# New engine sequences for a four-layer graph network kernel, and its bound checks moved into the planned graph

## The chip, the cores and the metric

The kernel runs on one core of a Trainium2 chip. The metric is the device time of one execution in microseconds; lower is better. The core has five engines that work side by side and meet through semaphores: PE (TensorE) multiplies matrices, DVE (VectorE) and ACT (ScalarE) do elementwise work, POOL (GpSimd) does small elementwise work and issues some DMAs, and SP (SyncE) issues the other DMAs. Each engine executes its own instructions in the order in which the program lists them. So the order in which the program is written decides who waits for whom.

## The reference

Sixteen batches of `x`, each 1024 nodes by 256 features in float32, and one `adj` matrix of 1024 by 1024 integers shared by all batches. Four layers, each with a norm in front and a residual:

```python
h = jnp.maximum(_layernorm(x, axis=-1), 0.0)
x = x + layer(h, adj, ...)

# layers 0 and 1: one-head graph attention
h = jnp.matmul(inp, W)
e = leaky_relu(e_src[:, :, None] + e_dst[:, None, :])     # e_src = h @ a1, e_dst = h @ a2
e = where(adj == 0, -1e9, e)
out = relu(softmax(e) @ h)                                # layer 1: elu, another slope

# layer 2: eight-head dot attention with the same mask, then
x = layernorm(x + t); f = relu(x @ w1 + b1) @ w2 + b2; x = layernorm(x + f)

# layer 3: graph attention with four heads of 64, elu
```

## The kernel before

The kernel has a fast path and a general path. The fast path computes softmax without subtracting the row maximum. It keeps track of extreme values while it works (`gat_seen`, `inv_seen`, `degree`, `below`); at the end it tests them against bounds, counts the broken ones into `bad`, and the program runs the general path only if `bad` is above zero (L2013 and L2014). With these inputs it is not run.

**Stages.** A stage is one layer of one batch. Stages are interleaved by a fixed list, so that a stage that needs much of DVE and ACT runs beside one that needs much of PE. In its steady part the list repeats layer 2 of batch b, layer 1 of b+1, layer 3 of b, layer 0 of b+2, once per batch.

**What a stage does.** `way_in` normalises a batch's rows, 128 nodes at a time, turns them on PE (`transpose_rows`, L1096 and L1099) and multiplies them by the layer's weights (`project`, L1103). Layers 0 and 1 (`gat_item`) form attention weights `p` on DVE (L1366) from a row `r`, a column `e` and the mask, and multiply them with the values `v` on PE (L1383, accumulator `av`). Layer 2 (`dot_item`) goes in groups of four heads by 128 keys by 512 queries: the scores on PE (`sc`, L1599), two exps on ACT (L1613), two multiplications by the mask on DVE (L1621), the values on PE (`acc`, L1630). The softmax sums need the weights of two groups added: a DMA that POOL issues adds one `pe` tile onto another in SBUF (`gather`, L1647, 1 MB), and PE sums the result (`totals`, L1660). Layer 3 (`pair_item`) forms two heads' weights at a time on DVE (L1445) and multiplies on PE (L1479 and, for the sums, L1503). After layer 2 comes `feed_forward`: for 128 nodes at a time DVE takes mean and variance (L1050, L1051), POOL adds epsilon and takes the power -1/2 in `root` (L1054, L1055, on 128 numbers), ACT scales (L1758), and PE turns and multiplies. `root` of the other norms is L1080 and L1081.

**Three forms of matmul.** Wide ones use the whole array (128*128: L1096, L1103, L1383). Scores use 32 rows and 128 columns (32*128), four heads beside each other. Values and sums of layers 2 and 3 use 128 rows and 32 columns (128*32).

**Memory.** Tiles sit in rings (`Ring`, `Hold`). PSUM has three places of two banks (`u`) and two of one bank (`acc`); one score group takes two of the `u` places. A ring's place comes free when the operations named in `ends` are done.

**The order.** Nothing is executed in the order in which the Python code creates it. Each piece of work is an `op` with an engine, a cost in microseconds, what it comes after, which ring places it takes and ends. The DMA queue of the gathers counts as a sixth engine, `QUEUE`. `forward` plays all operations on a model of the engines: at each step it takes the operation that can begin earliest, and among those within `SLACK` of 0.5 us the one with the lowest rank. The string `RANKS` holds one rank per operation, three characters each. The order in which the model plays is the order in which instructions are written out. A change of matmul form costs extra on PE (`SWITCH`), and `held` keeps a POOL operation from beginning while a DVE operation with two operands in SBUF runs:

```python
if o.eng == PE and o.form != form:
    cost, form = cost + SWITCH[o.form], o.form
if o.tiles:
    held[o.eng] = at + cost - BEFORE_END
```

SP's queue carries, in program order: the loads of `x` (`load_x`, L653), the edges of `adj` at the start (L724), the weights (L676), the rows `kept` (stored at L1312) and `r` (loaded at L1323 and L1327) of the graph attention stages, and the stores of the result (L1578). At the start ACT's queue carries the first layer's weights.

Of the kernel before, what the change touches and what calls it, by code (L numbers as in the profile page):

```python
# [26 lines left out]
F32 = mybir.dt.float32  # L27
BF16 = mybir.dt.bfloat16
U8 = mybir.dt.uint8
# [6 lines left out]
P = 128  # L36
# [11 lines left out]
    "#+;#TX#$I#U9#U3#&X#%h#WX#)4#Wc#&>#$b#U)##w##W$5o##o##Z##D##b#$'#$-##t##$#$:##r##y##G##Q#$F#$>#/4#$N#$R##x#%-#%^"  # L48
    "#$o#'S#'T#&F#&a#%g#&$#'%#&{##T#$|##?##@#%F#SZ##B#%+##>##S#$f##c##M##a##L##]##9##v##i##z##|##u##^#$@#$)##n#$0#$4"
    "##U#oi#-@##V#sX##F##X#$^##=##_#%e##P#)h##{#$<##q#$`#/3#$&#$P##m#$3#$8#$J#$,#$9#$K#$1#*e#%r##%##j#$a#&4$0;#Cy$0r"  # L50
    "#RB#Cx#%|#']#**#&@#)g#([#'q#%m#&]#&7#%v##8#$=##}#$G##-#$L#$_#$j#$M##)#$E##p#$]$$T#'?#%a$Mo#%5#$n#$U#%L#%9#%}#%R"
    "##(#$C#%%#$c#%8##Y#&L#%7#xt#%S#'V#]n#%l#$5$%C#%V#%E#0W#%0##l#&+#$i#&,#%n#(o#)v#)V#D,#%t#$v#$r#$S#%$#%##%'#$O#$d"
    "#$H#$6#)z##4#K5#$+#&I#%?#%Y#(8#YI#(A#<Z#$A#&;#$l#%x#&1#Au#$7#(s#%,#$;#%.#%T#%z#%O#&:#DW#d-#&Q#&A#)W#%s#'H#DU#'P"
    "#'E#&0#(2#(I#(4#'r#*d#e6#&=#,6#k8#&m$Fk$Pc#($#$x#>b#$w#$Z#%3#5Q#$T#&8$@{##J#%X##O#Gr#({#%:#'K#$h#&c#'8##,#&[#%="
    "#T+#$u#&`#V9#%&#'-#%*#JZ#SB#%/#%i##C##5#%w#us##2##H##N#$s#$.#$k##e##;#$e#')#%P#&l#%<##d#$*#$##vC#%K#XB#*|#$B#%G"
    "##A$/b#&6##1#%`#&D#((#%]#%I#%{#&%##0#%_#%Q#&9#&##&)#D=##7#FF$&r#&C#%d#&.##6#)0#&B#+4#O)##3##[#&Y#%@#&g#;b$&?#e'"
    "#4O#%2#&Z#&*#(y##/#%j$/i#&&#'&#di#&p#&/#&f#&M#&|#'.#('$5w#'*#(%#&N#$2#'6#&3#&d#&R#&K#&U#&o#&V##.#DD#&E#&q#M9#'="
    "#&<#&n#eH#'D#',#w'$0(#'X#'C#&z#'J#&h#'@$6t#U@#'[#';#'A#%;#(-#'x#a}#DE#kw#'W#%p#'_#N[#&r#(>#Sm#&u#)G$.4#)P$.3#&e"
    "$Ip#'d#ma#tD#);$Pa$Ph$PQ$K?#&i#'I#&s#'N#&v#'2#&j#%A$D+#&P#&H#0A#%k#(D$JC#'p#'>#'a#&x#&_$JO#G;#O/#'5#'L#%1#'k#0>"
    "$78#(P#ip#'e#'7#kv#P)#d`$Ms$1j#'g#(G#Pd#(l#)@#(E$?$#(c#0.#'w#'s#(p#'G#)E#'}#''#(^#(&#'|#(6#UK#(/$@J#'#$@O#'y#()"  # L60
    "#ku#$Q#'v#$/#Il#.W#B1#(:#(.$>1#)3#4/#Ix#4.#(5#(L$;V$>D##k#(1$9##'u#))#(d#)%#)^#*=#)_#)t##g#'R#'j#(##(,#'U#(9#'i"
    "#(n#(B#(V#(W#&'#(*#'m#*n#)8#)1#(}#;4#)y$$:#(x#C,#(i#(Y#(h#(_#(z#)m#(U#&?#)b#(g#(k#*K#(j$*_#(f#J@#*2#)F#Ah#,[$*9"
    "#*,#*7#-z#<c#)*$LG#)=#)<#++#)M#*:#-(#(v#)B#*+#)i#:q#*1#+9#2y#)?#)Q#+J#)D$$z#*3#,,#*}#)p#)U#;Y#'h#)a#$Y#+<#*9#)S"
    "#)[#*##)$#*&#*R#+%#*H#)w#*[#,r#->#*`#+-#.S#)(#)c#)O$$u#)#$+S#s|#)R#),#/M#)+#,f#*G#+H#*p#*c#(H#*%#*E#*8$,R#*a#*4"
    "#*V#*-#+0#Q5#*k#,U#*q#+*#*@#(@$OJ#*l#-$#*j#*M#)u#qU#+N#,B#*y#K%#-g#+L#*f#*O$P,#*N#*r#+(#*_#)n#,u#j{#-'#+5#+1#IV"
    "#*o#+f#*t$3%#,k#.##h6#+?#'1#-,#,I$2J#,j#+e#L}#,b#+x#+8$2)#E7#nl#kn#+O#+##+K#-D#S{#CK#+u#Oy#)l#,*#+>#+Y$<|#+V#CP"
    "#+t#+i#.M$6O#.C#sD#,$#sv$;[#,N#+`$C?#AC#-k#?L#,'#+z#,T#:M#+D#A<#,F#,>#Os#jT#,J#00#+{#g?#+|#)r#+q#+m#+/#*]#1F#,7"
    "#/[#*U#L^#,+#q<#+X#-+#,8#.`#,3#/)$-($E##-[$F@#D$#-a$8s#Hh#-w$*S$-z#-p#.B#E##-##.u#Ob$GE#F]#+C#8u#qs#.O#.T#-u#L+"
    "#-&#.e#;g#/1#,<#.*#ej#n.#)|#j7#,}#-{#.%#-B#]z#-S#-H#-E#-G#.2#)s$#Z#.(#.c#-Z#GY#a5#/G$Ng#-b#/g$Hu#,)#.i#=.#kT#A&"
    "#gi#,&$Ch#ef$D)$Kp#,Y#8h#-f#,i#,2#-t#*<$Cj#(|#,L#,1$Cs#yr#'0#.Z#,^#8g#/U#-2#,4#'<#/##/P$MP#,o#,Z#-m#ym#2H#g=#,{"  # L70
    "#*C#/d#-O#,]#-K#+&#.-#+W#-1#,l#+o#)o#.{#,##-<#,x#-i#+S#-I#-%#/Q#+}#01#)j#-F#-3#-l#.d#*w#.K#.h$;=$/D#-`#-?$F,#.]"
    "#,X#.g#,A#-_$F)$EL$FB$A=#-o#o8#.q#.&#-N$5r$EI$FC#._#-r#-e#W[#(w#.9#)x#-d#/J$/B#-:#,Q#WZ#}i$P7#)J#-Y#-s#9m#)X#2)"
    "#-7#.N#)`#KW#-U#'l#-V#-0#,?#-x#.I#RQ#,v#/?#.>#.$#.j#.'#.A#-}#.l#/%#.V#/o#.?#-X#./#.<#.b#05#/'#``#.=#-6#'(#+h#2|"
    "#MH#-8#.7#/e#.U#g)#/f#.x#15#/s#/2#.^#,K#/I#,W#,M#Ha$P`#g[#yg#,a#/`#.v#.Y#04#/q#/;#,m#/W#.X#+v#/@#+y$K>#+r#/b#It"
    "#,s#,t$'z#0r$GX#.:#,w#,_#,z#.8#+P#-;#9-#-J#-W#Yt#.m#0S#Ys$>x$(]#.y$9$#)f#+M#$[#(r#,5#*.#*)#,P#*?#*A#,R#$W#*F#*I"
    "#*J#*Q#*>#9e#*P#)9$Kf#+6#nk#+3#+'$3l$F0#+Q#*T#,D#(`#+,#,O#(;#+$#-A#,V#h/#-.#*^#*S#*g#*{$L{#)K$3Y#)T#+a#+n#+=$)E"
    "#+I#+g#+E#+2#+[#Ba#8G#,-#>R#)6#)5#+)#-|#,@$3n#.,#.R#.6#.J$N;#.H#.G#-n#.f#;y#/$#<&#1M#]b#/5#UU#/>#.Q#.t#).#`W#]T"
    "#/Z#zN#0+#-]#*z#/m#1%#/.$7:$Nv#/}#,H#1U$EV#/O#/E#Nt#/z$(B#0&#,:#,S#*$#D5#/u#0x#C/#0i#0{$-f$Mm#-v#u'$+[#'$#0M#0L"
    "#/_##'#N<#I[#.z#3w#):#0;$?F#0(#0P$8h#NP#DY$PU#/,$@X#/t#.}#::#YZ#+R#0'#0n#/h#/v#0F#+G#/=#HG#32#03#/j#C_#/i#-j#0I"
    "#/S#18#/^#/T#3?#.5#1C#z,#HS#0?#0o#6w$-0#1A#61#1k$;Q#1$#0u#0q#/y#/<#1m#1N#0m#/B#0<#0,#2L#26#0##0l#0J#0B#14#0|#/F"  # L80
    "#0]#0V#0[$+k#0O$+f#0a#3n#.+#/D#.w#06#/p#Xr#29#0H#0%#08#0)#0G#0`#0=#0Z#0:$Nn#0y#0k#0e#1,#KY#09#0d#0z#/A#2J#fr#-9"
    "#19$8`#2a#1_#sA#1B#0h#1D#1@#2=#2b#6u#1:#1`#1G#6v#7<#/K#0X#4I$+n#0/#1T#0g#1>#1-$+`#0b#1i#1e#2E#1o#/]$8q#4H#1=#3U"
    "#1}#/c$8K#sh#s?#0K#1W$)u#2C#21#+@#1p#1;#1f#1H#A*#1Q#16#1<#1j#1I#tY$*s#2q#2I#1O#1z#2w#1x$?9#3##/(#1t#1)#1+#1?#2<"
    "#3B#3&#ZZ#2Q#1l$I6#1h#2i#1c#2B#1q#4(#2/#2j#2m#2R$K;#6(#2t#2%#1J#2x#4'#3K#2K#Y1#0t#3c#57#/n#2W$-8#2$#3N#22#1L#3)"
    "#<O#/l#2c#2;#kZ#4D#2_#5A#3M#:u#2D#4F#27#1R#2+#<N#5@#3:#2S#<z$I0$?'#3F#4C#4b#0D#88#2{$Iv#2}#0Q#3>#z0#2z$O'$O&#3$"
    "#4>#39$'1#2e#:s#3/#3j#38#3e#3=#4k#35#4=#3J#5e#3h$5E#4|#Et#+d#*;#3a#2@#5Y#4x#3b#2,#1Z#3Q#4c#4q#79#5T#5'#11#4@#4d"
    "#66#7J#5F#4S#3d#3[#4a#4?#7E$L>#7)#4p#4W#4e#5($;1#;q#6k#5)#23#3+#5$#1n#4i#5d#4^#3y#5;#5^#6H#5h#4-$>P#'B#2'#0_#6h"
    "#0*#4+#3T#3-#<6#37#<v#1a#4g$/'#2##3_#3G#=+#Kb#2Z#{?#2d#4l#nv#2[#4,#2g#4n#:t#56#3W#4J#<r$:C#5>#1b#3(#3.#4L#I=#3{"
    "#N{#3g#l?#7T#59#1^#9;#SA$Iw#2:#58#30#64#13#6Y#12#2^$/*$-7#5i#3l#3Z#8x#2F#7/#1{#*X#3v#/k#1]#8|#1($:x#3`#]k#6]#2X"
    "$JG#2O#6X#2v#3X$9<$.q#2M#07#1[#5E#@Y$)i#tL#ie#40#3C#wv#34#02#3s#T'#3I#4v#3;#3i#2P#0w#5,#2V#x^#3p#77#3O#2]#6P#5P"  # L90
    "#4M$'S#43#7'#4U#0p$,{#4*#6'#3V#3}#3o#4y#5/#2r#5o#5n#5D#6S#3S#5}#5Z#6A#4K#50#5<#67#48#5B#3L#6:#3r#3D#3]#4;#3R#6%"
    "#+j#4f#5_#^{#5H#44#5:$--#4T#33#-R#81#5V#5p#7##^$#3H#41#8;#4t#6L#5y#4m#6-#62#6W#6Q#5k$PR#7N#53#5M#$q#83#2o#5|#2p"
    "#6{#yp$J/$$P#6t#7Q$J0#6M#5S$,]#3u#6s#7H#6+$&=#5`#6K#qc#54#4X#6}#74#|L#6d#Vy#4%#4$#3P#3x#aM#5-#4`#5L#yP#4j#46#j)"
    "#4:#4R#4Z$6p#4{$%>#4P#4z#4##6_#2f$:$#4h#4&#31#5K#4o#5U#6E$Cv#Fk#4w#5w$Np$2&#3f#4G#^z#5g#5m$8a#:T#68#6^#7?#4Y#5W"
    "#45#4E#47#|5$JS#}U$@H#8}#5[#5?$Be#6*#5O$-'#8D#5%#5v#78#5z#2u#9J#7`#6F#6/#6B#}|#5q#rq#70#Ld#87#6N#6J#7$#6r#3m#6x"
    "#+w#6$#6.#6o#76#yf#f>#6b#6l#ww#7(#6O#1S#5a#6f#7%#6e#6[#5f#1Y#7*#73#8-#5X#10#6>#7=#7@#7;#6;#1E#6m#7G#6?#7-#7d#7,"
    "#71#8V#6y#7k$@8#8_#82#91#8$#7l#7Z#7W#[S#7|#8L$51#8[#8I#8`#8i#8m$4M#8^#8W#8P#9,#9W#8c#8p#8##6D#:##8:#Yk#:R$Hn#9&"
    "#<@#9+$2_#;F$+q#V'$D6#8O#<<#?+#??#7S#7q#6U#7I#ET#7U#7]#5s#6j#7V#+p#5N#7b#7R#7}#9)#84#7c#8C#8F#8t#8&#7z#65#7s#7["
    "#7K#7X#7n#*x#6&#7w#7o#9*#7g#EK#8A#8%#6i$(D#7t#7L#6|#8<$&A#-C#8q#8X#,;#6z#8=#8R#8l#7m$J1#9$#>j#Ea#8(#6@#4V#rP#4B"
    "#?=#TB#7r#7P#80#8.#8k#9A#72#9=#8a#8z#9g#Dz#9r#8B#7p#:?#86#'O#9h$%U#:2#tM#-/#8b#8M#9:#:0#8n#9}#&-#Sz#.[#'9#9'#:1"  # L100
    "#t)#;|#(C#Y<#(X#8o#9b#9]#96#9N#9I#;p#9n#8/#8,#;Z#;9#=y#;P#:L#<,#;L#='#4}#9i#9<#9`#(q#=M#WJ#<|#94#(e#9D#9f#6q$Ot"
    "#6p$QC#6Z#:U#7>#9a#W@#:|#8r#m;#8Y#:(#95#9u#8]#:z#8s#9P#{.$(A#9x#=b#:*#7F#8Z#89#8j#9^#7^#8{#8Q#9T###$*-#;*#;8#>)"
    "#@f#>J#5u#@%#8S#7Y#>0#;z#:C#P-#98#;@#<B#9H$Ht#:-#7u#:p#:O#9@#(Z#:%#:=#:A$5b#:.#9V#75#;V#52$%J#zi$B'#:Y#9_##I$-`"
    "##<##&#:H#9t#9q#<V#9M$'J#:G#n]#:o#:c#&w#9U#:`#9/#:_#:Q#:9#9[#:]#8v#jt#:Z$3f$-&#?]#:y#'+#:@#k)#;H#k/#9p#:;#;'#)Z"
# [518 lines left out]
def fast_path(tc, bad, x, adj, l0_w, l0_a, l1_w, l1_a, w_qkv, ln1_g, ln1_b, ln2_g, ln2_b, w1, b1, w2, b2, l3_w, l3_a, out):  # L623
# [13 lines left out]
    with ctx:  # L637
# [128 lines left out]

        ops = []
        PE, DVE, ACT, POOL, SP, QUEUE = range(6)  # L770

        DELAY = (0.2, 0.12, 0.14, 0.06, 1.8, 1.9)
        ITSELF = 0.04

        SWITCH = {None: 0.2, 132: 0.21, 32: 0.125}


        BEFORE_END = 0.1
# [1266 lines left out]
```

## Time and profile before

| | |
|---|---|
| median of 3 runs | 4161.59 us (4154.62 to 4164.35) |
| the profiled execution | 4158.92 us |
| its span | 4157.2 us |
| mean granted PE clock | 0.996 |

The profile is of one execution. A row of a group gives line, engine, operation, what is written and read, the number of instructions, busy time and mean duration. In brackets of a timeline row stands how long the engine was idle before it and what ended that. Starts of matmuls are recorded and their ends are modelled, so neighbouring matmuls seem to overlap. Some groups that matter:

| line | what | count | mean ns |
|---|---|---|---|
| L1621 | DVE, mask on exps | 1024 | 1219 |
| L1613 | ACT, exp of scores | 1024 | 1022 |
| L1383 | PE, `av` of layers 0 and 1 | 4096 | 382 |
| L1599 | PE, scores | 4096 | 641 |
| L1630 | PE, values of layer 2 | 4096 | 604 |
| L1647 | POOL, issue of a gather | 256 | 883 |

A gather lands 8.8 us after its issue in the median.

### The profile page before, as it was taken

The page shows a single profiled execution, that of the slowest core. Times are in us where ns is not written, and L with a number is a line of the kernel's source. Part 1 is how long each engine was busy: PE and PEld are TensorE (multiplying, and loading weights), DVE is VectorE, ACT ScalarE, POOL GpSimd, SP SyncE. Part 2 cuts the span into 40 slices and gives each one's busy share as a digit, 9 for nine tenths or more (in the row PEclk, how much of TensorE's full clock was granted, in tenths as well). Part 3 has the DMA queues.
Part 4 walks back from the last instruction along what each step waited for, and adds up shares of the span by engine and source line. Part 5 has one row for each costly group of instructions (what it writes and reads, how often), then busy time and mean ns, then how long its engine had stood idle before and what let it go on. Part 6 is the DMA issues. An engine that isn't in the chain of part 4 may idle for free. (4 is left out here: it accounts for less than half of the span.)

```text
span 4157.2 us, 67132 instructions
## 1 busy us (share of the span) xinstructions
PE 4080.8 (98%) x25993; PEld 2150.9 (52%) x25993; DVE 3123.5 (75%) x5580; ACT 2316.4 (56%) x4235; POOL 1255.7 (30%) x2153
## 2 busy tenths in 40 slices
PE   8999999999999999999999999999999999999998
PEld 7735364553646535465454654546545465465433
DVE  7477867778676886767867678686787767859697
ACT  5564655646466464654646546475564655666452
POOL 3323141413324233142322423223232232423231
PEclk9999999999999999999999999999999999999999
DMA  3181814518155181641716317163271632736361
GB/s 126 25 174 32 188 37 107 108 47 173 37 128 107 36 163 42 140 89 47 152 42 145 84 45 154 42 146 83 51 148 42 144 85 58 146 83 126 74 141 47
DMA packets 106565, 398.91 MB, mean 96 GB/s; under 512 B 11272, under 2 KB 47488, under 8 KB 73472
## 3 DMA queue, kind: packets, MB, share of 16 engines
q0 software_dynamic: 46080, 302.01, 36.8%
q1 hardware_dynamic: 59744, 92.03, 6.6%
q8 instruction: 206, 3.38, 0.3%
q14 instruction: 119, 0.97, 0.1%
q10 hardware_dynamic: 416, 0.52, 0.0%
HBM read 107.87 MB, written 18.21 MB: 30 GB/s over the span
## 5 line engine op out<-in xcount | busy, mean ns | idle before, releaser
L1621 DVE TENSOR_TENSOR pe<-pe,mask 128x1024 f32<-128x1024 f32 x1024 | 1199.7, 1219 | 198.2 <-ACT pe L1613 195.0
L1613 ACT ACTIVATE pe<-sc 128x1024 f32<-128x1024 f32 x1024 | 996.6, 1022 | 299.8 <-PE sc L1599 252.6
L1383 PE MATMUL av<-v,p 128*128 128x257 f32 x4096 | 950.4, 382 | 10.5 <-ACT o L1406 6.8
L1383 PEld LDWEIGHTS av<-v,p 128*128 128x128 f32 x4096 | 758.8, 190 | 195.6 <-issue 59.1
L1445 DVE SCALAR_TENSOR_TENSOR p<-r,e,mask 128x1024 f32<-128x1024 f32 x512 | 622.5, 1274 | 100.3 <-DMA r<-kept 94.1
L1599 PE MATMUL sc<-qT,kT 32*128 32x512 f32 x4096 | 620.0, 641 | 6.8 <-ACT pe L1613 5.3
L1630 PE MATMUL acc<-pe,v 128*32 128x512 f32 x4096 | 535.7, 604 | 2.6 <-DVE pe L1621 1.9
L1647 POOL DMA_DIRECT2D pe<-pe x256 | 226.0, 883 | 980.9 <-PE acc L1630 667.2
L1080 POOL TENSOR_SCALAR rstd<-stats 128x1 f32<-128x1 f32 x512 | 157.8, 308 | 1039.4 <-ACT xn L1074 633.6
L1479 PE MATMUL acc<-p,v 128*32 128x512 f32 x4096 | 468.1, 593 | 0.0
L1599 PEld LDWEIGHTS sc<-qT,kT 32*128 32x128 f32 x4096 | 187.6, 183 | 387.5 <-ACT pe L1613 179.9
L1103 PE MATMUL pm<-l_wx,hT 128*128 128x259 f32 (+1 forms) x1536 | 368.4, 387 | 1.3 <-DVE y L1552 0.6
L1366 DVE SCALAR_TENSOR_TENSOR p<-r,e,mask 128x512 f32<-128x512 f32 x512 | 348.6, 743 | 15.3 <-DMA r<-kept 14.4
L1081 POOL TENSOR_TENSOR rstd<-rstd,minus_half 128x1 f32<-128x1 f32 x512 | 340.1, 664 | 42.6
L1103 PEld LDWEIGHTS pm<-l_wx,hT 128*128 128x128 f32 x1536 | 285.1, 190 | 82.9 <-issue 15.1
L1054 POOL TENSOR_SCALAR rstd<-stats 128x1 f32<-128x1 f32 x256 | 148.6, 580 | 465.0 <-DVE stats L1051 459.8
L1479 PEld LDWEIGHTS acc<-p,v 128*32 128x32 f32 x4096 | 131.3, 110 | 296.3 <-issue 280.6
L1660 PE MATMUL sums<-pe,pick 128*32 128x512 f32 x2048 | 270.5, 600 | 5.6 <-DMA pe<-pe 5.4
L1630 PEld LDWEIGHTS acc<-pe,v 128*32 128x32 f32 x4096 | 96.6, 108 | 337.7 <-issue 200.1
L1157 ACT ACTIVATE xn<-x,stats 128x256 f32<-128x256 f32 x256 | 125.8, 505 | 227.9 <-DVE stats L1051 223.1
L1503 PE MATMUL sums<-p,e 128*32 128x512 f32 x2048 | 249.3, 594 | 1.4 <-ACT v L1246 0.6
L1055 POOL TENSOR_TENSOR rstd<-rstd,minus_half 128x1 f32<-128x1 f32 x256 | 232.1, 907 | 21.4
(124 smaller groups left out, 4211.6 us busy)
## 6 DMA issues: line engine op xcount, KB each, us to landing
pe<-pe POOLq DMA_DIRECT2D x256, 1024.0 KB, 8.8
r<-kept SPq DMA_DIRECT2D x64, 512.0 KB
x<-in_x_dram SPq DMA_DIRECT2D x32, 512.0 KB
x<-offsets POOLq DMA_DIRECT2D x32, 512.0 KB, 5.3
y<-offsets POOLq DMA_DIRECT2D x32, 512.0 KB, 5.9
out_dram<-x SPq DMA_DIRECT2D x64, 256.0 KB
r<-kept SPq DMA_DIRECT2D x62, 256.0 KB
edges<-in_adj_dram SPq DMA_DIRECT2D x8, 512.0 KB
```

The lines of the kernel that those rows point to most:

```text
L1081: nc.gpsimd.tensor_tensor(rh.t, rh.t, minus_half, ALU.pow)
L1103: nc.tensor.matmul(dst, lhsT=lhsT[:, k, :], rhs=rhs[:, k, :], start=(k == 0), stop=(k == KC - 1))
L1366: nc.vector.scalar_tensor_tensor(ph.t[:, j % each, :], rh.t, s.e[:, j, H + h : H + h + 1], mask[:, j, cols], ALU.max, ALU.mult)
L1383: nc.tensor.matmul(avh.t[:, : s.hs + 1], lhsT=phs[part].t[:, j % each, i * P : (i + 1) * P], rhs=s.v[:, j, h, :], start=(j == 0), stop=(j ...
L1445: nc.vector.scalar_tensor_tensor(ph.t[:, hh, :], s.rh[hp].t[:, hh, :], s.e[:, j, col : col + 1], mask[:, j, :], ALU.max, ALU.mult)
L1479: nc.tensor.matmul(acc[n].t[(2 * hh + part) * W : (2 * hh + part + 1) * W, :], lhsT=s.v[:, jj, h, part * W : (part + 1) * W], rhs=p, start ...
L1503: both(lambda jj, n, hh, h, p: nc.tensor.matmul(sums.t[(2 * n + hh) * W : (2 * n + hh + 1) * W, 0, :], lhsT=s.e[:, jj, 2 * H + h : 2 * H + ...
L1599: nc.tensor.matmul(scs[pair].t[:, hh, :], lhsT=s.kh.t[r0 : r0 + D2, g, j * P : (j + 1) * P], rhs=s.qh.t[r0 : r0 + D2, g, cols], start=True ...
L1613: lambda pair=pair: nc.scalar.activation(part(pair), scs[pair].t, AF.Exp, scale=SCALE2),
L1621: lambda pair=pair: nc.vector.tensor_tensor(part(pair), part(pair), masks(), ALU.mult), [ex], tiles=True,
L1630: nc.tensor.matmul(head(acc, i), lhsT=s.v[:, j, g * QUAD + i, :D2], rhs=ph.t[:, i, :], start=(j == 0), stop=(j == NT - 1))
L1660: nc.tensor.matmul(head(sums, i), lhsT=pick[:, g, :], rhs=th.t[:, i, :], start=first, stop=last)
```

## The change

The change keeps every computation of the layers. It does five things.

1. `RANKS` is replaced as a whole, and `forward` reads it in another way: each engine, and the DMA queue, now executes its operations strictly in the order of the ranks. The model only merges the six sequences. All ranks of the new table are different whole numbers, 0 to 12288.
2. The model's times are changed: a change of form now depends on the form before and after and may pass while PE waits for something else; gathers, row loads, stores and some instructions have new durations. None of this issues an instruction. It is used where the ranks were found, and for the merging.
3. The load of batch 1's `x` is issued after four of the eight edge tiles instead of after all of them.
4. The bound tests become operations of the graph. Six DVE instructions each compare and count at once (`accum_out`), two more form the verdict, one matmul adds it over the partitions, and one DVE instruction copies it to `bad`. Before, these tests followed `play()`: twelve DVE instructions for the six tests, three for the verdict, the matmul and the copy.
5. The DVE instructions that note the extreme values are collected in `seen_ops`, so that the tests come after them.

```diff
 RANKS = (
...
             nc.sync.dma_start(out=edges[t // 2][:, t % 2, :], in_=adj[t * P : (t + 1) * P, :])
-        load_x(1)
+            if t == TH - 1:
+                load_x(1)
...
-        DELAY = (0.2, 0.12, 0.14, 0.06, 1.8, 1.9)
+        DELAY = (0.2, 0.12, 0.14, 0.06, 1.8, 0.6)
...
-        SWITCH = {None: 0.2, 132: 0.21, 32: 0.125}
+        GATHER_OP, QUEUE_BIG, QUEUE_SMALL = 1.0, 5.7, 2.9
+        LAG, ROW_ONE, ROW_FOUR = 0.38, 4.2, 4.8
+        SWITCH = {
+            (0, None): 0.0, (0, 32): 0.0, (0, 132): 0.0, (132, 32): 0.23, (132, None): 0.2, (32, 132): 0.095,
+            (32, None): 0.115, (None, 132): 0.1, (None, 32): 0.12,
+        }
...
-        def forward(rank):
+        def forward(rank, in_order=True):
...
+            turns = [deque(sorted((o for o in ops if o.eng == eng), key=lambda o: rank[o.number])) for eng in range(6)]
...
-                at = ready[o.number]
+                at = ready[o.number] + o.lag
                 if o.eng == POOL or o.tiles:
                     at = max(at, held[POOL + DVE - o.eng])
+                if o.eng == PE and o.form != form:
+                    at = max(at, time[PE] + SWITCH[form, o.form])
...
+                if in_order:
+                    open_ops = [[turn[0]] if turn and not missing[turn[0].number] else [] for turn in turns]
                 at, o = choose(open_ops, time, begin, rank, SLACK)
+                if in_order:
+                    turns[o.eng].popleft()
                 cost = o.cost
-                if o.eng == PE and o.form != form:
-                    cost, form = cost + SWITCH[o.form], o.form
+                if o.eng == PE:
+                    form = o.form
...
-                        SP, 0.4, rank + 4.0 + part, lambda hh=hh, load=load: load(hh), [room],
-                        delay=3.6 if H == 1 else 4.2,
+                        SP, 0.55, rank + 4.0 + part, lambda hh=hh, load=load: load(hh), [room],
+                        delay=ROW_ONE if H == 1 else ROW_FOUR,
...
-            issued = op(POOL, 0.9, at[0] - 4.0, gather, [valued] + ready + masked, delay=0.6)
-            gathered = op(QUEUE, 5.6, at[0] - 4.0, lambda: None, [issued], ends=[ph])
+            issued = op(POOL, 0.9, at[0] - 4.0, gather, [valued] + ready + masked, delay=GATHER_OP)
+            issued.lag = LAG
+            gathered = op(QUEUE, QUEUE_BIG, at[0] - 4.0, lambda: None, [issued], ends=[ph])
...
-        edges_in = [arrival(9.0 + 1.35 * t) for t in range(NT)]
+        edges_in = [arrival(10.2 + 1.28 * t + (2.7 if t >= TH else 0.0)) for t in range(NT)]
...
+        def verdict(seen_ops, checks, rank):
+
+            def count(i, seen, bound, within):
+                held = small.tile([P, 3 * B], F32, tag="held", name="held", bufs=1)[:, : seen.shape[1]]
+                nc.vector.tensor_scalar(held, seen, bound, 0.0, within, ALU.add, accum_out=ok[:, i : i + 1])
+
+            return [op(DVE, 0.26, rank + i, lambda i=i, c=c: count(i, *c), seen_ops) for i, c in checks]
...
+        judged = op(DVE, 0.32, at - 32.0, judge, counted)
+        counth = banks("count")
+        summed = op(
+            PE, 0.15, at - 31.0,
...
+            ), [judged], takes=[counth],
+        )
+        op(DVE, 0.12, at - 30.0, lambda: nc.vector.tensor_copy(bad, counth.t[:1, 0, :1]), [summed], ends=[counth])
         play()
-
-
-        checks = ((gat_seen[:, 0, :], GAT_HIGH, ALU.is_le), (gat_seen[:, 1, :], GAT_LOW, ALU.is_ge),
...
-        for i, (seen, bound, op) in enumerate(checks):
...
-            nc.vector.tensor_scalar(held, seen, bound, None, op)
-            nc.vector.tensor_reduce(ok[:, i : i + 1], held, AX.X, ALU.min)
...
-        nc.tensor.matmul(count[:1, :1], lhsT=broken[:, 0:1], rhs=broken[:, 1:2], start=True, stop=True)
-        nc.vector.tensor_copy(bad, count[:1, :1])
```

## The prediction

> **What bounds the kernel now.** I read the page's first two parts, the waits of TensorE, the windows of equal stretches, and then timelines of places where TensorE stood still.
>
> ```profile
> span 4157.2 us, 67132 instructions
> PE 4080.8 (98%) x25993; PEld 2150.9 (52%) x25993; DVE 3123.5 (75%) x5580; ACT 2316.4 (56%) x4235; POOL 1255.7 (30%) x2153
> ```
>
> TensorE is the bound: 98% against DVE's 75%. Its idle time is 4157.2 - 4080.8 = 76.4 us. That is not all that an order can win: a row by row count hides what it costs to change the shape of matmul. The timeline of TensorE alone shows it:
>
> ```profile
> 1519.71 1.04 PE L1630 MATMUL acc<-pe,v 128*32 128x512 f32 x8
> 1520.68 1.14 PE L1599 MATMUL sc<-qT,kT 32*128 32x512 f32 x8
> ...
> 1536.76 1.06 PE L1660 MATMUL sums<-pe,pick 128*32 128x512 f32 x8
> 1537.64 1.04 PE L1630 MATMUL acc<-pe,v 128*32 128x512 f32 x8
> 1538.50 1.04 PE L1660 MATMUL sums<-pe,pick 128*32 128x512 f32 x8
> ```
>
> Starts count here (ends are modelled and overlap). Eight 128*32 matmuls followed by the same form take 0.88 and 0.86 us; followed by the 32*128 form of the scores, 0.97: a change of form costs about 0.1 us. Every one of 512 score groups is entered and left, so there are over 1000 changes, some 100 us and more, all inside "busy".
>
> The windows, cut at the instructions of L1725 (one per batch), give twelve stretches with the same work, a batch of each layer. Columns: length, busy time of each engine, with counts, granted clock, DMA share, GB/s.
>
> ```profile
> 539.10:792.80 253.70, 251.10 (x1615) 132.38 (x1614) 192.06 (x338) 141.00 (x257) 77.66 (x131) 1.00 0.44 96
> 792.80:1048.90 256.10, 254.71 (x1627) 134.83 (x1626) 193.87 (x346) 145.38 (x270) 76.17 (x137) 1.00 0.44 95
> ...
> 2851.20:3114.40 263.20, 257.81 (x1623) 134.42 (x1622) 193.83 (x345) 145.14 (x265) 81.09 (x134) 0.99 0.43 93
> ```
>
> They last from 539.1 to 3627.4, 257.4 us each in the mean. Length minus TensorE busy is 2.6, 1.4, 1.6, 3.9, 3.9, 4.6, 4.6, 2.0, 3.4, 5.4, 1.8 and 1.0: 36.1 us. The rest of the 76.4: first 50 us 11.6, 330.3 to 539.1 5.7, 3849.1 to 4084.3 3.8, the last 72.9 us 17.0, elsewhere 2.2.
>
> The worst single stop is worth following:
>
> ```profile
> 2288.19 5.21 POOL L1055 TENSOR_TENSOR rstd<-rstd,minus_half 128x1 f32<-128x1 f32 x1
> ...
> 2288.34 4.63 DVE L1621 TENSOR_TENSOR pe<-pe,mask 128x1024 f32<-128x1024 f32 x4
> ...
> 2293.43 0.51 ACT L1758 ACTIVATE y<-y,rstd 128x256 f32<-128x256 f32 x1 [4.11 <-POOL rstd L1055]
> ...
> 2294.91 2.08 PE L1599 MATMUL sc<-qT,kT 32*128 32x512 f32 x4 [3.26 <-ACT pe L1613]
> ```
>
> An instruction on 128 numbers (median 0.58 us) takes 5.21 beside four DVE instructions with two SBUF operands; ACT, in order, waits 4.11 for it with an exp queued behind, and TensorE 3.26. L1054 shows the same (5.30 us at 2803, 4.23 at 3069).
>
> **The change part by part.**
>
> *Bound checks into the graph.* Now they run after everything:
>
> ```profile
> 4144.41 0.69 DVE L1565 TENSOR_TENSOR x<-x,y 128x512 f32<-128x512 f32 x1
> 4145.02 0.18 DVE L1996 TENSOR_SCALAR held<-gat_seen 128x48 f32<-128x48 f32 x1
> ...
> 4148.29 0.15 DVE L2004 CAST bad<-count 1x1 int32<-1x1 f32 x1 [0.37 <-PE count L2003]
> ```
>
> ```profile
> L2041 POOLq DRAIN  x3: 40/107/6726, 4149.3 to 4156.9; - x3
> ```
>
> The last useful DVE instruction ends at 4145.10; 15 small ones and a matmul follow until 4148.44, then every engine loads the flag and branches, and POOL drains for 6.73 us until 4156.0; the program ends at 4157.15. In the diff the last nine ranks of the new table stand at 12174 to 12214 of 12288, 75 places and more before the end, so the flag is there before the last stores. POOL has nothing left by then, so load, branch and drain lie under the last matmuls. What is late next: DVE reaches its last barrier (L2014, 4152.7) 4.3 us after the flag; counted from 4145.10 this is 4149.4. SP had issued the last store by 4146.06, and its packets ended by 4148.5. From DVE's barrier SP took 0.3, the closing exchange 0.8: end near 4150.6. Gain 6.5; at least 3.3 (the checks alone) if the drain cannot start early. I take 6.5. The eight remaining DVE instructions of about 0.2 us and one cast lie in a stretch where DVE is busy 53.5 of 72.9 us; the matmul adds about 0.3 us to TensorE. Without that cover they would cost 1.9 us.
>
> *x of batch 1 loaded after four of eight edge tiles.* No bytes more; its two DMAs on SP's queue (1.66 us of issue) move ahead of four edge DMAs, which land up to 2.7 us later (the shift that the diff gives them). They feed masks first needed by the second half of the first stage, behind eight value groups of 1.74 us (the diff's figure; the trace has 1.91 at its start). After 16.2 us TensorE stops in this head for 0.15 us only. I take 0; 2.7 if that cover is gone, and not a gain, as TensorE has no wait there.
>
> *New costs in the planner* (switch table, `LAG`, `GATHER_OP`, row loads) issue nothing; they act only through the order.
>
> *The order.* All five engines and the DMA queues get new sequences; every instruction stays, each gather's issue on POOL, each row load and store on SP included. Four terms:
>
> (a) Waits that the planner can see. The best three stretches idle 1.0, 1.4 and 1.6, 1.3 in the mean. Twelve at 1.3 would give back 36.1 - 16 = 20. But TensorE's list of waits has "tp <- ACT y L1758: 10.0, 8 times", and with the 3.26 above 13.3 us come from stretched POOL instructions, which the planner does not know. Left: 7. The two odd stretches can give 5.7 + 3.8 - 2.6 = 7. Sum 14.
>
> (b) Changes of form. TensorE's busy time per matmul record is 0.1555 to 0.1560 us in the best three of the twelve, 3052.2/19469 = 0.1568 over all. At 0.1558 the twelve would save 19 us, of which 8.5 is clock (below): 10. The new table makes the pass scores, wide matmuls, narrow ones, scores cheaper (0.20 + 0.12 + 0.095) than the reverse (0.23 + 0.115 + 0.1), where the old one charged 0.535 for both; a search that sees this can win more. Bounds: -5 (it buys fewer waits with more changes) to 30.
>
> (c) Stretched POOL instructions: 13.3 us of waits. Here a rule speaks against this change. The Trainium skill, SBUF — State Buffer, "Who interferes with whom": a DVE instruction with two SBUF inputs contends with a GpSimd instruction that reads SBUF, and the second one blocks until the first is done. That is one L1621, 1.22 us, and it is what `held` in the planner does before and after. Above, the wait ran over four of them. By the rule the planner sees these waits and the search can give back all 13.3; by the trace it does not, and a new order draws them anew. The measurement decides: 4 (some fall away because DVE's trains change), bounds -25 to 13.
>
> (d) Clock. Windows cut at three stops show TensorE at half rate:
>
> ```profile
> 2294.90:2301.70 6.80, 6.79 (x28) 2.87 (x32) 4.38 (x4) 4.11 (x5) 1.12 (x2) 0.50 0.87 167
> 2810.20:2813.60 3.40, 3.40 (x20) 0.88 (x18) 2.10 (x2) 2.49 (x3) 1.14 (x3) 0.52 1.09 285
> 3076.60:3083.40 6.80, 6.80 (x18) 2.08 (x17) 6.80 (x9) 2.81 (x3) 1.01 (x2) 0.50 0.94 175
> ```
>
> 17.0 us at half rate lose 8.5. The stops before them were 3.26, 2.74 and 1.67 us. The Trainium skill, TensorE: Matmul & The Clock Gate, "HAM oscillation — how this bites in real kernels", allows idle gaps up to about 3.4 us; by that none of these costs clock and the term is 0. By the trace it is tied to (c): I take 3 of 8.5.
>
> DVE's own waits for row loads (94.1 us at L1445, 14.4 at L1366) I cost at nothing: TensorE's list has 0.6 us for DVE's p. If a row load slips behind a blocked store on SP (SP waited 491.1 us for L1565 ahead of stores), DVE stops, its masks behind it, and TensorE within about two score groups.
>
> Sum: 6.5 + 0 + 14 + 10 + 4 + 3 = 37.5. The profiled execution took 4158.92, 1.7 over its span; 4158.9 - 37.5 = 4121.4. The median of the three runs is 2.7 above the profiled one. Between 4121.4 and 4124.1 I say 4123.
>
> **The rivals.**
>
> *Only the tail counts.* The search finds nothing that the chip honours: waits move instead of going. For it: the old order already fills TensorE to 98%, and (c) is unknown to both. Against: equal stretches differ by up to ten us. Then 4161.6 - 6.5, about 4155, between 4145 and 4159. This is also the case in which the change does not do what it says.
>
> *More stretched POOL instructions: slower.* Place: `root` at L1054 and L1055 in the feed-forward of each layer 2, four per half batch, 128 in all. Price: the three worst stops cost 3.26 + 2.74 + 1.67 us and 8.5 of clock, 5.4 each. An order that packs DVE tighter puts more of them beside trains of four L1621. It cancels the gain from 37.5 / 5.4 = 7 more such stops on; at 10 more the time is 4123 + 54 = 4177, slower than before. For it: L1055 waits in 21 cases already (30.7 us at L1758). Against: three of 128 are that bad now, in an order that did not avoid them either.
>
> **How the numbers follow.** Forecast, the order gains too: 0.66, all faster, its own range 4085 to 4145. Only the tail: 0.22, half below the line and half within it. Slower by POOL: 0.12, of which 0.01 lands within. A measurement of this kernel tells about 0.2%, 8.3 us, from no change (the three runs lie 9.7 apart). Faster 0.77, within 0.12, slower 0.11. The range runs from 4085 (term (b) at 30 and (c), (d) in full: 6.5 + 20 + 30 + 13 + 8.5 = 78) to 4163, which takes in the tail case and leaves out most of the slower one.
>
> **What would show it.** Right: no DVE instruction of the checks after the last L1565, and end minus last L1565 5 to 6 us instead of 12.05; TensorE idle 45 to 60 us; equal stretches near 254.5 us; few windows at clock 0.50. Wrong: the drain still behind the last store; L1054 or L1055 above 3 us in more than six cases; sums L1660 waiting for DMA pe<-pe beyond today's 5.4 us, as a gather takes 6.9 to 13.7 us to land and the planner reckons with one figure; stretches as uneven as now, which would say that waits only moved.

## The result: slower, by 0.8%

| | before | after |
|---|---|---|
| median, runs on one chip | 4158.26 us, 4 runs (4154.62 to 4164.35) | 4192.66 us, 4 runs (4185.57 to 4194.90) |
| ratio | 1 | 1.0078, 95% interval 1.0059 to 1.0098 |
| profiled execution; its span | 4158.92; 4157.2 us | 4185.57; 4183.6 us |
| TensorE idle in the span | 76.4 us | 93.5 us |
| TensorE at half rate before the tail | 17.0 us in 3 places | 57.8 us in 13 places |

The forecast was 4123, range 4085 to 4163. Half rate stands for stretches in which the granted clock is 0.50; the tail is the stretch after the last matmuls. The line numbers of the changed kernel are 16 or 17 higher from the planner on: scores L1615, exp L1629, mask L1637, `acc` L1646, gather L1663, `sums` L1677, `av` L1399, DVE's `p` L1382 and L1461, `root` L1070 and L1071, loads of `r` L1339 and L1343, stores L1594.

The page of the changed kernel, its span and first part:

```profile
span 4183.6 us, 66898 instructions
PE 4090.1 (98%) x25993; PEld 2155.2 (52%) x25993; DVE 3082.4 (74%) x5580; ACT 2278.2 (54%) x4235; POOL 1261.4 (30%) x2153
```

TensorE is still 98% busy, and that hides two opposite movements. 57.8 us at half rate lose up to 28.9, where 17.0 lost 8.5; so busy time grew by 9.3 us although up to 20.4 were added by the clock, and the work itself came down by some 11. Idle time rose by 17.1 although the end after the last matmul became 5.4 us shorter.

The waits of TensorE, changed kernel (total, times, longest):

```profile
PE sums L1677 <- DMA pe<-pe: 20.1, 19, 2.1
PE acc L1646 <- DVE pe L1637: 11.9, 4, 5.0
PE sc L1615 <- ACT pe L1629: 10.8, 6, 3.4
...
PE tp L1112 <- ACT y L1775: 6.9, 4, 3.8
PE av L1399 <- DVE p L1382: 5.1, 1, 5.1
```

Before, the first of these was 5.4 us, the second 1.9, and the last did not exist. These rows, with the half rate behind them, make up most of the result: `sums` waits for gathers that have not landed, and `acc` and `av` for DVE, which itself waits for a DMA. The same waits in the kernel before:

```profile
PE sums L1660 <- DMA pe<-pe: 5.4, 9, 1.9
PE acc L1630 <- DVE pe L1621: 1.9, 3, 0.8
```

And DVE's waits for the 256 KB rows of the one-head layers, before and changed:

```profile
DVE p L1366 <- DMA r<-kept: 14.4, 3, 6.4
```

```profile
DVE p L1382 <- DMA r<-kept: 44.3, 7, 13.0
```

One place shows how, in the timeline (start, length, engine; in brackets the idle time ahead and what ended it):

```profile
992.35 2.01 SPq L655 DMA_DIRECT2D x<-in_x_dram  x2
...
994.40 1.67 SPq L1339 DMA_DIRECT2D r<-kept  x1
...
999.36 1.06 PE L1677 MATMUL sums<-pe,pick 128*32 128x512 f32 x8 [1.03 <-DMA pe<-pe]
...
1006.57 1.06 PE L1677 MATMUL sums<-pe,pick 128*32 128x512 f32 x8 [1.84 <-DMA pe<-pe]
...
1017.67 0.75 DVE L1382 SCALAR_TENSOR_TENSOR p<-r,e,mask 128x512 f32<-128x512 f32 x1 [9.64 <-DMA r<-kept]
...
1021.41 1.66 PE L1646 MATMUL acc<-pe,v 128*32 128x512 f32 x8 [3.40 <-DVE pe L1637]
```

SP issues 1 MB of `x` and right behind it a row load of 256 KB, in the middle of a train of 1 MB gathers. The row's packets end 22.8 us after its issue. DVE stands 9.64 us with the masks queued behind the row's first use, and TensorE stops for a mask that has nothing to do with the row. Then the clock drops. The windows at two such stops (length, busy times, granted clock, DMA share, GB/s):

```profile
1021.70:1025.10 3.40, 3.40 (x20) 0.87 (x16) 3.40 (x4) 0.00 (x0) 0.85 (x1) 0.51 0.57 116
3824.10:3830.90 6.80, 5.93 (x22) 2.50 (x23) 2.14 (x3) 0.58 (x1) 0.85 (x1) 0.50 1.06 263
```

The stretches that hold one batch of each layer are as uneven as before. Cut at a batch's last `sums` of layer 2, three of the changed kernel's twelve:

```profile
775.00:1038.60 263.60, 256.43 (x1627) 133.29 (x1619) 190.13 (x339) 142.26 (x264) 76.79 (x135) 0.99 0.44 99
...
2072.60:2340.00 267.40, 256.65 (x1627) 133.51 (x1619) 190.94 (x340) 141.28 (x263) 74.98 (x135) 0.99 0.41 87
...
2601.10:2852.40 251.30, 249.87 (x1611) 130.47 (x1603) 187.03 (x330) 137.48 (x249) 76.02 (x125) 1.00 0.45 99
```

The good one has 1.4 us of idle time, the bad ones 7.2 and 10.8. Over the twelve the mean is 259.3 us, against 257.1 before with the same cut.

The second source of stops is the one that the prediction knew:

```profile
3331.45 7.64 POOL L1070 TENSOR_SCALAR rstd<-stats 128x1 f32<-128x1 f32 x1
...
3332.11 6.90 DVE L1637 TENSOR_TENSOR pe<-pe,mask 128x1024 f32<-128x1024 f32 x6
...
3339.88 0.51 ACT L1775 ACTIVATE y<-y,rstd 128x256 f32<-128x256 f32 x1 [4.96 <-POOL rstd L1071]
...
3341.34 1.13 PE L1615 MATMUL sc<-qT,kT 32*128 32x512 f32 x4 [3.40 <-ACT pe L1629]
```

0.36 us in the median, 7.64 beside six masks in a row. Roots above 3 us: 8, against 4 before.

### The profile page after: what moved, and what is told of

The parts are those of the page before. It is cut to its first block, busy times and chain, and to the rows that moved or that the text cites. A ratio compares the mean times of both kernels' runs of the same rounds, so it can differ in the third digit from the quotient of the medians.

```text
span 4183.6 us, 66898 instructions
## 1 busy us (share of the span) xinstructions
PE 4090.1 (98%) x25993; PEld 2155.2 (52%) x25993; DVE 3082.4 (74%) x5580; ACT 2278.2 (54%) x4235; POOL 1261.4 (30%) x2153
## 3 DMA queue, kind: packets, MB, share of 16 engines
q0 software_dynamic: 46080, 302.01, 36.4%
## 5 line engine op out<-in xcount | busy, mean ns | idle before, releaser
L1637 DVE TENSOR_TENSOR pe<-pe,mask 128x1024 f32<-128x1024 f32 x1024 | 1200.2, 1218 | 175.7 <-ACT pe L1629 173.3
L1629 ACT ACTIVATE pe<-sc 128x1024 f32<-128x1024 f32 x1024 | 1003.2, 1022 | 351.6 <-PE sc L1615 297.4
L1399 PE MATMUL av<-v,p 128*128 128x257 f32 x4096 | 951.9, 383 | 8.8 <-DVE p L1382 5.1
L1399 PEld LDWEIGHTS av<-v,p 128*128 128x128 f32 x4096 | 760.2, 190 | 197.9 <-issue 57.1
L1461 DVE SCALAR_TENSOR_TENSOR p<-r,e,mask 128x1024 f32<-128x1024 f32 x512 | 625.7, 1274 | 96.3 <-DMA r<-kept 92.7
L1615 PE MATMUL sc<-qT,kT 32*128 32x512 f32 x4096 | 619.5, 644 | 11.8 <-ACT pe L1629 10.8
L1646 PE MATMUL acc<-pe,v 128*32 128x512 f32 x4096 | 548.4, 611 | 12.9 <-DVE pe L1637 11.9
L1663 POOL DMA_DIRECT2D pe<-pe x256 | 225.9, 882 | 1033.6 <-PE acc L1646 690.9
L1096 POOL TENSOR_SCALAR rstd<-stats 128x1 f32<-128x1 f32 x512 | 162.9, 318 | 1026.1 <-ACT xn L1090 616.0
L1382 DVE SCALAR_TENSOR_TENSOR p<-r,e,mask 128x512 f32<-128x512 f32 x512 | 356.8, 742 | 52.8 <-DMA r<-kept 44.3
L1615 PEld LDWEIGHTS sc<-qT,kT 32*128 32x128 f32 x4096 | 185.6, 184 | 403.0 <-issue 166.7
L1097 POOL TENSOR_TENSOR rstd<-rstd,minus_half 128x1 f32<-128x1 f32 x512 | 332.8, 650 | 42.7
L1070 POOL TENSOR_SCALAR rstd<-stats 128x1 f32<-128x1 f32 x256 | 174.1, 680 | 535.3 <-DVE stats L1067 533.5
L1677 PE MATMUL sums<-pe,pick 128*32 128x512 f32 x2048 | 273.5, 608 | 20.6 <-DMA pe<-pe 20.1
L1646 PEld LDWEIGHTS acc<-pe,v 128*32 128x32 f32 x4096 | 94.4, 109 | 338.5 <-issue 212.1
L1416 DVE RECIPROCAL inv<-av 128x1 f32<-128x1 f32 x256 | 41.7, 164 | 263.9 <-PE av L1399 256.5
L1119 PE MATMUL pm<-hT,qkv_sb 128*128 128x512 f32 x512 | 228.8, 594 | 1.0 <-ACT hT L1115 0.6
```

The costliest lines, as they stand in the source:

```text
L1097: nc.gpsimd.tensor_tensor(rh.t, rh.t, minus_half, ALU.pow)
L1119: nc.tensor.matmul(dst, lhsT=lhsT[:, k, :], rhs=rhs[:, k, :], start=(k == 0), stop=(k == KC - 1))
L1382: nc.vector.scalar_tensor_tensor(ph.t[:, j % each, :], rh.t, s.e[:, j, H + h : H + h + 1], mask[:, j, cols], ALU.max, ALU.mult)
L1399: nc.tensor.matmul(avh.t[:, : s.hs + 1], lhsT=phs[part].t[:, j % each, i * P : (i + 1) * P], rhs=s.v[:, j, h, :], start=(j == 0), stop=(j ...
L1461: nc.vector.scalar_tensor_tensor(ph.t[:, hh, :], s.rh[hp].t[:, hh, :], s.e[:, j, col : col + 1], mask[:, j, :], ALU.max, ALU.mult)
L1615: nc.tensor.matmul(scs[pair].t[:, hh, :], lhsT=s.kh.t[r0 : r0 + D2, g, j * P : (j + 1) * P], rhs=s.qh.t[r0 : r0 + D2, g, cols], start=True ...
```

## Experiments

Three theories. **D**: the sequences lose on DMA landings, gathers and row loads, that come later than the planner's one figure. **P**: they lose on stretched GpSimd roots. **T**: what the search gained is small or not there at all. Ratios are to the kernel before on the same chip (its median was 4157 to 4164 us on the different chips); microseconds beside them are the ratio times 4158.3.

### The checks alone

The kernel before with the new check code and nine more ranks; no other operation changes its place.

```diff
-        play()
...
-        nc.vector.tensor_copy(bad, count[:1, :1])
+        counted = verdict(seen_ops, list(enumerate((
...
+        play()
```

> The kernel before, with one part of the change alone: the bound checks as nine operations of the graph near the end; every other instruction keeps its place on its engine. If the tail term of the prediction is right, the time falls by 5 to 6.5 us, to about 4152, and the end comes 5 to 6 us after the last L1565. If the checks in the graph get into DVE's way at the end, it stays at 4158 or more. Together with the changed kernel it also tells what the sequences alone cost: with 5.7 us gained at the tail they would have cost 34.4 + 5.7 = 40 us.

Measured: 4153.18 us, ratio 0.9984 (0.9976 to 0.9992), -6.7 us. Its span ends 6.48 us after the last L1566, 12.05 before; 5 to 6 were expected. The tail term is right to about 1 us. The rest of the change therefore costs 32.4 + 6.7 = 39 us. This is also the fastest version of the full computation that was run, ahead of both kernels.

### Row loads ahead of x and stores

The changed kernel, SP's sequence alone altered. The new sequences put stores and loads of `x` between the write of `kept` and the loads of `r`; before, they never stood there.

The edit is in the table `RANKS`; 24 stores and loads of `x` change places. Written out in words for one place (`room` marks a free place in a ring and issues nothing), first the changed kernel, then this run:

```text
SP: kept, room, row, x, row
SP: kept, room, row, row, x
```

> The changed kernel with SP's sequence alone altered: the row loads of a layer's sources (r <- kept) go ahead of 24 stores and x loads that the new sequence puts between them and the write of kept, as the sequence of before has it. Theory D (waits on DMA landings): row loads that come behind x on SP land up to 30 us after their issue, against 8.7 at most before; DVE and then TensorE stop for them. Then the row load stops go (11.8 us in three places with up to 8.5 us of half clock behind them): 4172 to 4182. Theory P (stretched GpSimd instructions in the way of ACT): nothing changes, 4189 to 4196. If x loads and stores that now come later are waited for, it is slower than 4193.

Measured: 4178.53 us, ratio 1.0042 (1.0028 to 1.0056): 15 us less than the changed kernel. The same place in its timeline:

```profile
983.47 1.60 SPq L1339 DMA_DIRECT2D r<-kept  x2
...
1004.35 1.81 SPq L655 DMA_DIRECT2D x<-in_x_dram  x2
...
1010.16 0.75 DVE L1382 SCALAR_TENSOR_TENSOR p<-r,e,mask 128x512 f32<-128x512 f32 x1 [3.00 <-PE acc L1646]
```

Both rows go out together, `x` 21 us behind them, and DVE no longer waits for a row there. From the packets in the traces, loads of 256 KB rows ended at most 8.7 us after their issue before, 29.9 in the changed kernel, 22.0 here. So the order on one DMA queue, which the planner valued at nothing, was worth 15 us, with an interval of about 10 us either way (an estimate from the two intervals). `sums` still waits 18.4 us for gathers, half rate is no less (58 us), and the one row load that took 22.0 us still stops DVE for 13.1 us. The two profiles cannot show where the 15 us went: they are 4.4 us apart in span, since the one here is of the slowest of its five runs and that of the changed kernel is of the fastest of its four.

### Gathers of a quarter, in both kernels

```diff
-    out=th.t.rearrange("p i q -> p (i q)"), in_=ph.t.rearrange("p i q -> p (i q)"), accum_op=ALU.add
+    out=th.t[:, 0, :], in_=ph.t[:, 0, :], accum_op=ALU.add
```

> The kernel before with gathers of a quarter of their size: three of the four heads' planes are left out of the accumulation, so the softmax sums of layer 2 are of part of the scores only. Both theories: TensorE's waits of sums for the gather (5.4 us) go, and the time falls by 5 to 10 us, to about 4150. It is the partner of the next run.

> The changed kernel with gathers of a quarter of their size, the same part left out. Theory D: the waits of sums for the gather (20.1 us in 19 places) go, with part of the half clock behind them, and row loads land sooner because the DMA engines are freer: 25 to 40 us less, 4153 to 4168, so that it comes within 12 us of its partner. Theory P: it falls as little as its partner does, to about 4185, and the distance of 34 us stays.

Measured: before 4146.51, ratio 0.9968 (0.9956 to 0.9981), -13.3 us, a little more than expected. Changed kernel 4128.85, ratio 0.9922 (0.9906 to 0.9939), -32.4 us: that is 64.8 below its full form, more than D expected, and the order of the two kernels turns round. Full gathers cost the new sequences 51.5 us more than the old ones, with about 12 us either way (an estimate from the intervals). It is not GpSimd's own time that the edit saves: issuing a gather takes 0.88 us in the mean in the changed kernel and 0.89 in its quarter form. What changes is the landing. In the view of DMA issues (KB each, median us to landing), the kernel before, the changed kernel and then its quarter form:

```profile
pe<-pe POOLq DMA_DIRECT2D x256, 1024.0 KB, 8.8
```

```profile
pe<-pe POOLq DMA_DIRECT2D x256, 1024.0 KB, 8.2
```

```profile
pe<-pe POOLq DMA_DIRECT2D x256, 256.0 KB, 3.3
```

Between the two profiled spans (4183.6 and 4134.3, 49.3 apart) these waits and the clock account for most: `sums` 20.1 to none, `acc` for DVE 11.9 to 1.5, `av` for DVE 5.1 to none, 35.6 together (other waits grew, and idle time fell by 31.9 in all); half rate 57.8 to 37.4 us, another 10.2. The longest 256 KB row load fell from 29.9 to 11.8 us with SP's order as it was. The gathers thus cost by being late themselves and by making other DMAs late.

The lateness has a shape. In the changed kernel the median landing was sooner than before (8.2 us, 8.8 before) and the median `sums` started 4.4 us after its gather had landed (2.7 before). But the tail is longer: one landing in ten took over 12.0 us (10.5), the longest 16.3 (13.7), and 31 of 256 `sums` started within 0.3 us of the landing (19). Gathers issued with two or more DMAs of GpSimd still under way took 11.7 us in the mean (10.6).

### Roots that only write, in both kernels

```diff
-                nc.gpsimd.tensor_scalar(rh.t, mh.t[:, 1:2], EPS, None, ALU.add)
-                nc.gpsimd.tensor_tensor(rh.t, rh.t, minus_half, ALU.pow)
...
+                nc.gpsimd.memset(mh.t[:, 1:2], 1.0)
+                nc.gpsimd.memset(rh.t, 1.0)
```

> The kernel before with GpSimd's root of stats_of (one over the standard deviation, in layer 0 and in the first norm of the feed-forward) replaced by two memsets that only write: the division by the deviation is left out there. Every wait for it stays, but GpSimd has nothing to read from SBUF in it. If stretched roots cost as the traces show (stops of 13.3 us next to them and up to 8.5 us of half clock), the time falls by 10 to 20 us, to 4138 to 4148; if memsets are stretched as well, or the stops have other causes, it stays at 4155 or more. Partner of the next run.

> The changed kernel with the same part left out. Theory P, now as a second part beside theory D (gathers and row loads late): stretched roots stand next to stops of some 24 us in the changed kernel, with 14 us of half clock, so 25 to 40 us less: 4153 to 4168, that is some 15 us more than the partner gains. If D alone explained the loss, both kernels would gain the same.

These memsets also shorten a root that was not stretched, so a second pair writes 180 and 360 more numbers of a spare tile and keeps the plain duration:

> As the run of the kernel before with memsets for the roots of stats_of, but with two longer memsets into a spare tile ahead of them, so that a root again takes about 0.9 us of GpSimd, writing only: the division by the deviation is left out there as well. If stretching was the loss, 4141 to 4145, as with the short memsets; if it was the plain duration, 4155 or more.

> The same in the changed kernel. If stretching was the loss, 4163 to 4168, as with the short memsets (4163.4); if it was the plain duration, back to 4185 or more.

Measured: before 4141.70, ratio 0.9951 (0.9935 to 0.9968), and with the long memsets 4137.02, ratio 0.9952 (0.9937 to 0.9967): -20 us both times. Changed kernel 4163.40, ratio 1.0001 (0.9992 to 1.0010), and 4161.40, ratio 1.0010 (1.0003 to 1.0017): -32 and -28 us. So it is not the duration, it is the stretching that costs: 20 us in the old order, and 8 to 12 more in the new one. That surplus hangs on the four runs of the full changed kernel, whose own interval is 8 us wide to either side; where gathers are a quarter (below) it is 17.5, and clearer: on one chip the two kernels lie 17.7 us apart with their roots and 36.4 without them, and the runs of each of the four forms lie within 8.1 us. P is real, and too small to explain 39. The short memsets came out where they were expected, the long ones 2 to 4 us below. (256 roots go through these two lines, half of them in layer 0; those of the other norms still read, and one took 5.16 us in the changed kernel with the memsets.) The durations (min/median/max ns), long memsets and then the changed kernel:

```profile
L1071 POOL MEMSET spare<- x256: 241/248/590, 1.5 to 4056.5; 128x180 f32 x128
L1073 POOL MEMSET spare<- x256: 398/398/403, 7.6 to 4058.4; 128x360 f32 x128
```

```profile
L1070 POOL TENSOR_SCALAR rstd<-stats x256: 211/362/7637, 7.6 to 4083.0; 128x1 f32<-128x1 f32 x128
L1071 POOL TENSOR_TENSOR rstd<-rstd,minus_half x256: 567/570/5199, 7.9 to 4083.6; 128x1 f32<-128x1 f32 x128
```

### Both left out, in both kernels

The two edits above together: quarter gathers and short memsets.

> The kernel before with gathers of a quarter and roots as memsets, both parts left out. Worked out from the run with quarter gathers (4146.5; stops of 10.7 us next to stretched roots, 3.4 us of half clock lost): 4132 to 4137.

> The changed kernel with both parts left out. In its run with quarter gathers (4128.9) every stop of 1 us or more except one at the start had a stretched root beside it: 26.8 us, and 14.2 us lost at half clock. If P is the rest, 4088 to 4100, 35 to 45 us below its partner: the gain that the forecast expected of the new order, once the two things that the planner does not know are out of the way. If the stops have another cause, about 4125.

Measured: before 4129.90, ratio 0.9922 (0.9906 to 0.9939), -32.4 us; changed kernel 4093.48, ratio 0.9834 (0.9818 to 0.9850), -69.0 us. The first is 2 us below what was expected, the second inside. All four corners, in us against the kernel before:

| | old sequences | new sequences and checks | difference |
|---|---|---|---|
| full | 0 | +32.4 | +32.4 |
| roots write only (short memsets) | -20.4 | +0.4 | +20.8 |
| gathers of a quarter | -13.3 | -32.4 | -19.1 |
| both | -32.4 | -69.0 | -36.6 |

T falls. Without the two disturbances the change gains 36.6 us, some 6 of them by the checks. The pages, old sequences and then new:

```profile
span 4127.7 us, 67131 instructions
PE 4069.1 (99%) x25993; PEld 2147.9 (52%) x25993; DVE 3121.2 (76%) x5580; ACT 2313.7 (56%) x4235; POOL 905.0 (22%) x2153
```

```profile
span 4092.2 us, 66881 instructions
PE 4054.1 (99%) x25993; PEld 2154.6 (53%) x25993; DVE 3079.2 (75%) x5580; ACT 2281.4 (56%) x4235; POOL 937.9 (23%) x2153
```

Busy time falls by 15.0 us, idle time by 20.5 (58.6 to 38.1), of which 5.4 to 5.6 are the tail; neither has any half rate before the tail. And the equal stretches are even, 253.5 us in the mean:

```profile
767.30:1020.90 253.60, 252.60 (x1623) 132.88 (x1619) 190.02 (x339) 142.33 (x264) 54.89 (x135) 1.00 0.23 53
...
2292.10:2546.80 254.70, 253.81 (x1635) 134.87 (x1627) 192.82 (x351) 144.43 (x273) 57.83 (x137) 1.00 0.21 44
```

### Sequences with margins

Can the gain be had with the full computation? In four versions operations were moved along their engines, in the kernel's own model, with landings and roots assumed later than the planner's figures. Two start from the rows-first order, two from the old sequences with SP's left alone. The edit is the table `RANKS` and nothing else:

```diff
-RANKS = (
+RANKS = (
...
```

> The changed kernel with other sequences and nothing else: starting from the rows-first order (4178.5), single operations were moved along their engines where that lowered 0.4 times the planner's own end plus 0.6 times its end with every gather and offset landing 1.5 us later, every row load 3 us later and every root of stats_of 0.8 us later. Theory D and P: the order lost because it left no margin for landings and roots that come later than the planner's one figure; with margin, most of the 18 us of sums waiting for gathers and part of the stops beside roots go, with their half clock: 4135 to 4160, so faster than before (4158). If margins don't help, because a late landing delays everything behind it whatever the order, it stays at 4170 to 4180.

> The same with wider margins (2.5, 4 and 1.5 us, weights 0.3 and 0.7) and fewer moves (some 1700 operations stand elsewhere, against some 7300). By D and P it keeps more room behind the gathers, but the search got less far: 4145 to 4170. If only the number of moves matters, it stays near 4178.

> The changed kernel with other sequences and nothing else: those of before with the nine operations of the checks in them, SP's left as it is, and some 1700 operations moved along their engines where that lowered 0.4 times the planner's end plus 0.6 times its end with gathers and offsets landing 2 us later, row loads 4 us later and roots 1.5 us later. If the missing margin is the cause of the loss, a search that keeps one should gain on the chip: 4125 to 4148, below the kernel with the checks alone (4153). If fixed sequences from this planner lose whatever the margin, 4155 to 4180.

> The same search run to a lower end (some 7700 operations stand elsewhere; the planner's end lower by 17 us and its end with margins by 19 us than in the run before this). With margin as the cause, 4110 to 4140; if every move makes stretched roots and late landings likelier whatever the margin, above the run before this.

Measured: s2 4186.95, ratio 1.0064 (1.0050 to 1.0078); s4 4170.38, ratio 1.0030 (1.0021 to 1.0038); o1 4164.16, ratio 1.0016 (1.0008 to 1.0023); o3 4163.51, ratio 1.0016 (1.0010 to 1.0023). None came out where missing margin as the cause would have put it, except s4, 0.4 us above the upper edge of its range (4145 to 4170); s2 is slower than any outcome that was named, and o1 lies where it was expected if fixed sequences from this planner lose whatever the margin, and why it is 13 us slower than the checks alone stays open. In s2 the search put row loads behind `x` and stores again: one behind `x` took 36.5 us to land, and single stops reach 12.3 us. In o3 `sums` waits only 4.4 us for gathers and rows land within 13.0 us, so D is mostly gone; but 10.1 us of stops of 1 us or more stand beside stretched roots (one root took 9.74 us), 20.4 us before the tail are at half rate, and TensorE's busy time less the half rate, 4087.6 - 10.2 = 4077.4 us, is no lower than in the kernel before (4080.8 - 8.5 = 4072.3): this search did not lower the busy time. A margin of 1.5 to 4 us for landings and 0.8 to 1.5 us for roots was not enough, and no full version that keeps the gain was found. A model that knows the stretching was not tried.

## Why the prediction was wrong

**Tail: right to about 1 us.** 6.5 forecast; 5.6 in the spans with the checks alone, 5.4 in the changed kernel, 6.7 by the ratio. The end came 6.6 us after the last DVE instruction, where 5 to 6 were expected.

**Head: nearly right.** No gain was forecast; its first 50 us idle 10.0 us, 11.6 before.

**(a) and (b): right in size, and not to be seen in the time; for (b) the mechanism is not shown.** 14 and 10 were forecast. With both disturbances out, idle time without the tail fell by 15 and busy time by 15. Changes of form explain little of the busy time: in the traces they only fell from 1399 to 1379, and at the planner's own prices those of the new order cost 204 us and those of the old one 207. Nor do the traces show the dearer direction that the prices assume: with both disturbances out, from the start of the last of the scores to the start of the next matmul it is 0.518 us in the median, be that a wide or a narrow one (priced 0.20 and 0.23). What the other 12 us are stays open, so the good size of (b) is in part luck.

**(c): wrong in sign, inside its bounds.** A gain of 4 was taken; the stretching cost 8 to 12 us more than in the old order, part of it by the clock (with the memsets, half rate before the tail fell from 57.8 to 30.7 us, in the old order from 17.0 to none). The doubt that stood beside it (-25 to 13) was the right one. The rule of the Trainium skill, SBUF — State Buffer, "Who interferes with whom", that a GpSimd instruction which reads SBUF waits until a DVE instruction with two SBUF inputs is done, is half borne out: instructions that only write stayed at 0.77 us at most, but the reading one waited for six DVE instructions, not for one.

**(d): wrong in sign.** 3 us less was forecast, up to 20.4 more were lost in the profiled executions. It follows the stops, as the prediction said; the stops grew. The rule of idle gaps up to some 3.4 us (The Trainium skill, TensorE: Matmul & The Clock Gate, "HAM oscillation — how this bites in real kernels") again allowed too much: see the last section.

**The step that failed: DMA landings were put at nothing.** The prediction costed DVE's row loads at nothing because TensorE waited 0.6 us for them in the old order, and gave the gathers no term at all. Both readings were of an order in which row loads stood straight behind `kept` on SP. The sentence beside it ("If a row load slips behind a blocked store on SP, DVE stops, its masks behind it, and TensorE") describes what happened, and the last paragraph named `sums` waiting for DMA as what would prove it wrong; neither was carried into the sum, the rivals or the range. Gathers of full size, with the row loads that they delay, cost the new order 51.5 us more than the old one, more than the whole forecast gain. The slow rival had the right shape, more stops and half rate behind them, but its mechanism was given 54 us and was worth 8 to 17.5: with the gathers a quarter and the roots as they are, the new order is still 19.1 us ahead of the old one.

**The signs named.** No check instruction behind the last L1581: seen. Roots above 3 us in over six cases: 8. `sums` waiting beyond 5.4 us: 20.1. TensorE idle 45 to 60 us: 93.5, and 38.1 with both disturbances out. Stretches near 254.5 us: 259.3, and 253.5. The lower end of the range, 4085, lies 1 to 4 us above what the sum of 78 beside it gives.

## What to carry to other kernels

An order that a search had packed to a model's figures turned the spread of landings, which the model lacked, into stops; so ask of each DMA how late it may land, not how long it takes. When an order is replaced, compare it queue by queue with the old one: what stood next to what on the DMA queue was worth 15 us here and had no price in the model. A factorial of two suspected costs, each left out of both kernels, showed a gain of 36.6 us (some 6 of it the checks) that the result itself hid completely.

## What the runs showed of the hardware

- Half rate goes with stops of TensorE shorter than 3.4 us too, and not by a sharp limit. Over the sixteen profiled kernels, without the first and last 20 us: all 43 stops of 3 us or more have a half rate stretch beside them (within 8 us), 21 of 27 between 2 and 3 us, 17 of 151 between 1 and 2. In o1 a single stop of 0.90 us stands ahead of one. Each stretch before the tail lasts 3.4 us or a multiple.
- A root of 128 numbers was held for 9.74 us beside a train of DVE masks (o3), 7.64 in the changed kernel; writes alone 0.77 us at most.
- A 256 KB row load, 2.3 us at its fastest, took up to 36.5 us behind other transfers of SP's queue while gathers ran (s2).
